# Two of the four channel-mix down products computed by two levels of the seven-product scheme

## The chip, the cores and the metric

The kernel runs on one core of a Trainium2 chip. The metric is device time in microseconds, the median of several executions. TensorE (PE in the profile) multiplies, VectorE (DVE) adds, subtracts and normalises, ScalarE (ACT) does activations and copies out of PSUM, GpSimd (POOL) and SyncE (SP) mostly issue DMAs here.

## The reference, cut to what matters

The input is 2048 tokens of 512 features, in float32. The reference does a layer norm and then an RWKV layer: a time mix (four 512x512 products) and a channel mix, followed by a feed-forward part (FFN).

```python
kk = (h * cm_mk + hh * (1 - cm_mk)) @ Wkey.T     # 512 -> 2048
kv = jax.nn.silu(kk) @ Wval.T                    # 2048 -> 512, the channel mix's down product
sr = jax.nn.sigmoid((h * cm_mr + hh * (1 - cm_mr)) @ Wcr.T)
x = x + sr * kv
...
gate_up = jnp.einsum('bsh,oh->bso', h_shard, w_gate_up)
gate, up = jnp.split(gate_up, 2, axis=-1)
out = jnp.einsum('bsi,hi->bsh', silu(gate) * up, w_down)   # the FFN's down product
```

## The kernel before, in words

The tokens are cut into four blocks of 512 (`b` = 0 to 3). For each block the time mix and the channel mix run first, for all blocks; only then comes the FFN, again block by block. The residual of each block goes through device memory (`resid`) between the two parts.

**The scheme.** A product of two 512x512 matrices is done on 2x2 blocks of 256 with seven block products in place of eight (a Strassen-Winograd scheme). It needs four sums of the weights' blocks (S1 to S4) and four of the activations' blocks (T1 to T4). `unit` (L526) does this: each of its `product` calls issues four 128x256 matmuls per weight, and `unit` has seven products. `down_unit` (L977) is such a unit with four weights (WVAL to WVAL+3), since the inner dimension is 2048: 7 x 4 x 4 = 112 matmuls of 128x256. `down_product` (L1114), used by the FFN's down product alone, goes a second level down: each of the seven products (steps n = 0 to 6, `DOWN`) is itself split in quarters of 128 and done by seven products of four 128x128 matmuls, so 7 x 7 x 4 = 196 matmuls. Its operands need sums of quarters of the activations (`quarter_sums`, L1103: four subtractions of 128x512 per step, in the order T1, T2, T4, T3), and the results are put together from `u` tiles by `rest`, `seventh` and `summed`. In a step the order of the products is: A11, A12, then S2 with T2 (`third`), S4, S1 with T1 (`fifth`), S3 with T3 (`sixth`), A22 with T4 (`seventh`). `sixth` and `seventh` are put off and issued between the first products of step n+1.

**Weight sums.** `prepare` (L143) loads four pieces of a weight to SBUF through GpSimd's queue, makes four sums on VectorE and stores them to scratch in device memory. The list of such items (`preps`: `early`, then WK, WR, WV, WO, then `late`) is worked off a little at every `tick`, as `credit` allows. Weights and sums reach TensorE through SyncE's queue and a ring of 12 tiles (`ring`).

**What sets the order.** The program writes out the order of TensorE, VectorE and ScalarE by hand. Each engine runs its own instructions strictly in that order. After each product `tick` (L290) adds `SHARE` = 0.88 of the product's time to a budget, `slack`, from which the costs of VectorE's instructions (`cost`: 0.135 us and 1.07 ns per element of a partition) are taken; while the budget is positive, `tick` issues one more piece of pending work: a weight sum, else a step of the `hot` queue (sums of activations), else of the `background` queue (norms and mixes). Work that belongs to a product, such as putting a result together, is issued with that product whatever the budget. If a product needs something that hasn't been issued, it is issued on the spot (`need`, L314, or `run_one(True)`). `ffn_in` (L1006) is one of the background items: it makes the input of the FFN's block: four residual adds, the moments, a reciprocal root by Newton steps, four scalings, transposes on TensorE, four sums. For block 0 it is pushed just before the last `down_unit`.

The activations of the channel mix's down product lie in separate tiles of 128x2x256 (`q_tile`), one per group `g` of 512 hidden features; those of the FFN's lie in one tile for all four groups, so that a quarter sum there is one instruction for four groups.

Of the kernel before, what the change touches and what calls it, by code (L numbers as in the profile page):

```python
# [9 lines left out]
F32 = mybir.dt.float32  # L10
# [10 lines left out]
HB = TB // 2  # L21
EPS = 1e-5
PLAIN = 2
WAIT = 5
# [35 lines left out]
def rwkv_ffn_kernel(  # L60
# [3 lines left out]
    vecs: bass.AP,  # L64
    w: bass.AP,
    wd: bass.AP,
    out: bass.AP,
# [11 lines left out]
    up = ctx.enter_context(tc.tile_pool(name="up", bufs=6))  # L79
    small = ctx.enter_context(tc.tile_pool(name="small", bufs=3))  # L80
    ps = ctx.enter_context(tc.tile_pool(name="ps", bufs=6, space=bass.MemoryType.PSUM))
    pv = ctx.enter_context(tc.tile_pool(name="pv", bufs=1, space=bass.MemoryType.PSUM))
# [5 lines left out]
    htp = mixes.enter_context(tc.tile_pool(name="htp", bufs=2))  # L88
    prep = mixes.enter_context(tc.tile_pool(name="prep", bufs=6))
    pools = {"q": mixes.enter_context(tc.tile_pool(name="qp", bufs=30))}  # L90

# [27 lines left out]
    for n in range(NW):  # L119
        sources[n], sums[n] = parts(n), scratch(f"sum{n}", 4)  # L120
    for k in range(4):
        sources["d", k] = [wd[q, k] for q in range(4)]
        sums["d", k] = scratch(f"d{k}", 4)
    for q in (A11, A12, A22, S1, S2, S3, S4):
        sources["dd", q] = [wd[q, k] if q < 4 else sums["d", k][q - 4] for k in range(4)]
        sums["dd", q] = scratch(f"dd{q}", 4)

# [15 lines left out]
    def prepare(n, own):  # L143

        raw = []
        for k in range(4):
            t = prep.tile([P, 2, HB], F32, tag="raw", name="raw") if own else q_tile("q")
            paced(nc.gpsimd.dma_start(flat(t), sources[n][k]))
            raw.append(t)
        yield 1  # L150
        a11, a12, a22, a21 = raw
        for k, o, i0, i1, op in (
            (0, a22, a21, a22, ALU.add),
            (2, a21, a11, a21, ALU.subtract),
            (1, a11, a22, a11, ALU.subtract),
            (3, a12, a12, a11, ALU.subtract),
        ):
            tt(o, i0, i1, op)
            nc.gpsimd.dma_start(sums[n][k], flat(o))
            yield  # L160

    def ring(src):
        t = wring.tile([P, 2, HB], F32, tag="w", name="w")
        nc.sync.dma_start(flat(t), src)
        return t
# [6 lines left out]

    def down_weight(q, k):

        if k >= 4:
            need_sums(("dd", q))
            src = sums["dd", q][k - 4]
        elif q >= 4:
            need_sums(("d", k))
            src = sums["d", k][q - 4]  # L180
        else:
            src = wd[q, k]
        return ring(src).rearrange("p a (h c) -> p (a h) c", c=P)
# [64 lines left out]
    def prep_one():  # L248
        item = preps[0]
        if item[1] > 0:  # L250
            return False
        try:
            if next(item[2]) is not None:
                item[1] = WAIT
        except StopIteration:
            preps.popleft()
            finished.add(("sums", item[0]))
            if len(preps) > 1 and item[3] > 1:
                begin(preps[1])
            elif preps:  # L260
                begin(preps[0])
        return True
# [7 lines left out]
    def prepare_all(ns, own, depth):  # L270
        empty = not preps
        for n in ns:
            preps.append([n, 0, prepare(n, own), depth, False])
        if empty:
            for item in list(preps)[:depth]:
                begin(item)

    def need_sums(n):
        while ("sums", n) not in finished:
            begin(preps[0])  # L280
            preps[0][1] = 0
            prep_one()

    def due():
# [672 lines left out]
    def up_unit(b, g):  # L957
# [3 lines left out]
        def sink(i, j, c):  # L961
            t = q_tile("s")
            nc.scalar.activation(t, c, AF.Silu)
            s[i, j] = B[(B11, B12, B21, B22)[2 * i + j]] = t

# [11 lines left out]
    def down_unit(b):  # L977
# [6 lines left out]
        def done():  # L984
            nc.sync.dma_start(resid[b], x1s.pop(b))

        unit(
            [WVAL + g for g in range(4)],
            [Lazy((b, g)) for g in range(4)],
            sink,  # L990
            True,
            done,
            loose=b == NB - 1,
        )

# [51 lines left out]
    def ffn_up(b, g):  # L1047
        s = gated.pop((b, g))
        hid = hidden.setdefault(b, {})

        def sink(i, j, c):
            q = (B11, B12, B21, B22)[2 * i + j]
            if q not in hid:
                hid[q] = hidden_tile()
            tt(hid[q][:, g], c, s[i, j], ALU.mult)
            if g == 3:
                made.add((b, q))
                if q in (B11, B22):
                    quarter_sums(b, 0 if q == B11 else 1)

        def done():
            if g == 0:
                for t in (T1, T2, T4):
                    hid[t] = hidden_tile()
            urgent((b, "f", g), sums_of({t: hid[t][:, g] for t in hid}))
            if g == 3:
                made.update((b, t) for t in (T1, T2, T4, "T3"))

# [4 lines left out]

    hidden, made, asked = {}, set(), set()
    room = {}
# [5 lines left out]
    def last_room():  # L1081

        room["hidden"] = ctx.enter_context(tc.tile_pool(name="hidden", bufs=7))
        pools["q"] = ctx.enter_context(tc.tile_pool(name="fq", bufs=15))
        more = ctx.enter_context(tc.tile_pool(name="more", bufs=1))
        m, _ = op_tile("quads")
# [4 lines left out]

    def quarters(t):
        return {2 * k + m: t[:, :, k, m * P : (m + 1) * P] for k in range(2) for m in range(2)}

    def quarter_operand(b, n):

        x = quarters(hidden[b][DOWN[n][1]])
        new = room["sets"][n % 2]
        x[T1], x[T2], x[T4] = new[:3]
        x["T3"] = new[3] if n < 2 else x[B12]  # L1100
        return x

    def quarter_sums(b, n):  # L1103
        x = quarter_operand(b, n)
        asked.add((b, n))

        def run():
            for o, i0, i1 in (T1, B12, B11), (T2, B22, T1), (T4, B21, T2), ("T3", B22, B12):
                tt(x[o], x[i0], x[i1], ALU.subtract)
                yield  # L1110

        urgent((b, "quarters", n), run())

    def down_product(b, sink, final):  # L1114
        base = {}

        def summed(n, r):
# [28 lines left out]
            else:  # L1146
                add("u2", "u2")
                sink(1, 0, base["u2"])

        def steps(n):  # L1150
# [3 lines left out]
            st = {}  # L1154
            x = quarter_operand(b, n)

            def product(dst, q, k, first):
                if k in (T1, T2, T4, "T3"):
                    while (b, n) not in asked:
                        flush_one()  # L1160
                    while (b, "quarters", n) not in finished:
                        run_one(True)
                wt = down_weight(a, q)
                for g in range(4):
                    mm = nc.tensor.matmul(  # L1165
                        dst,
                        lhsT=x[k][:, g, :],
                        rhs=wt[:, g, :],
# [42 lines left out]
            def seventh():  # L1211
# [3 lines left out]
                if n + 2 < 7:  # L1215
                    quarter_sums(b, n + 2)
                summed(n, r)
# [4 lines left out]
        for n in range(7):  # L1222
            t = DOWN[n][1]
            while (b, t if t != T3 else "T3") not in made:
                flush_one()
            one = steps(n)
# [6 lines left out]
            for k in range(2, 5):  # L1233
                one[k]()
                tick(half)
                if n == 0:
                    pop_held()
            held.extend((half, k) for k in one[5:])

    def ffn_down(b):  # L1240
# [12 lines left out]

        down_product(b, sink, final)

    early = [WCR] + [WKEY + g for g in range(4)] + [WVAL + g for g in range(4)]
    late = [n + g for g in range(4) for n in (WG, WU)] + [("dd", A11)]
    late += [("d", k) for k in range(4)] + [("dd", q) for q in (S4, S2, A12, S1, S3, A22)]  # L1260

# [27 lines left out]
    for b in range(NB):  # L1289
# [6 lines left out]
        if b + 1 < NB:  # L1296
            out_unit(b + 1)
        need((b, "ck"))
        if nxt:
            push(f"norm{b + 2}", time_norm(b + 2))  # L1300
        for g in range(4):
            up_unit(b, g)
            if b == 1 and g == 0:
                credit[1] = 0.55
            if g == 0:
# [14 lines left out]
        if nxt:  # L1320
            for n, u in (("k", k_unit), ("r", r_unit), ("v", v_unit)):
                u(b + 2)
    while preps:
        need_sums(preps[-1][0])
    mixes.close()
    last_room()
    for b in range(NB):
        for g in range(4):
# [16 lines left out]
def _layout(inputs):  # L1345
# [30 lines left out]
    )  # L1376
    def quarter_quarter(i, j, m, k):
        at = slice(i * HB + m * P, i * HB + (m + 1) * P)
        lo = j * HB + k * P

        q = [down[at, g * H + lo : g * H + lo + P].T for g in range(4)]
        return np.stack(q, axis=1).reshape(P, 4 * P)

    places = ((0, 0), (0, 1), (1, 1), (1, 0))
    wd = np.stack(
        [np.stack([quarter_quarter(i, j, m, k) for m, k in places]) for i, j in places]
    )
    return {
        "x": x,
        "vecs": np.ascontiguousarray(vecs),  # L1390
        "w": np.ascontiguousarray(w),
        "wd": np.ascontiguousarray(wd),
    }
# [19 lines left out]
```

## Time and profile before

| | |
|---|---|
| median of three runs | 1256.66 us (1255.7 to 1257.06) |
| profiled execution, time / span | 1256.11 / 1254.3 us |
| PE busy | 1238.0 us, 99% |
| DVE busy | 702.6 us, 56% |
| ACT busy | 355.8 us, 28% |
| channel mix's fourth down product (`down_unit(3)`) | about 627 to 679 us from the start, other units' matmuls between |
| FFN | from 679 us |
| FFN's down product of block 0 | about 774 to 823 us |

An fp32 matmul stands in the records as two matmul instructions, so counts of records are halved to get matmuls. In a timeline a line is: start in us, duration in us, engine, source line, operation, output<-input, count, and in brackets how long the engine sat idle before and what released it.

### The profile page before, as it was taken

Reading aid. Unit: us, or ns where it says so; the run is one execution under the profiler, and the core shown is the slowest. Engines: PE = TensorE matmul, PEld = TensorE weight load, DVE = VectorE, ACT = ScalarE, POOL = GpSimd, SP = SyncE. Lnnn points to the kernel's source line nnn. Section 1 sums busy time; section 2 is a strip of 40 time slices with the busy share of each in tenths; the row PEclk is TensorE's granted clock in tenths of the full one; section 3 lists DMA queues with packets and bytes.
Section 4 is the critical chain, followed back from the end, with each engine's and each line's share of the span. In section 5 each row is a group of like instructions: output and inputs, shape, how many; then the busy total and the mean of one; then the engine's idle time right before and its main releaser. Section 6 shows DMA issues by size and latency. Waiting matters only on the chain.

```text
span 1254.3 us, 18161 instructions
## 1 busy us (share of the span) xinstructions
PE 1238.0 (99%) x6588; PEld 1109.2 (88%) x6588; DVE 702.6 (56%) x1319; ACT 355.8 (28%) x656; POOL 151.1 (12%) x276
## 2 busy tenths in 40 slices
PE   8999999999999999999999999999999999999998
PEld 7888888888888888888888888998899988998898
DVE  5867566467674665722562265555546455462466
ACT  5433263142522334302311232212221132212211
POOL 2122221222121222222210000000000000000000
PEclk9999999999999999999999999999999999999999
DMA  5666777888778877798865655895559855785575
GB/s 188 233 195 211 244 249 244 249 292 282 241 259 257 290 251 248 248 334 309 254 211 178 221 145 151 247 345 164 144 173 302 280 151 150 234 291 165 152 220 200
DMA packets 137959, 288.55 MB, mean 230 GB/s; under 512 B 17296, under 2 KB 18320, under 8 KB 136848
## 3 DMA queue, kind: packets, MB, share of 16 engines
q1 hardware_dynamic: 115424, 215.53, 56.1%
q0 software_dynamic: 21440, 70.27, 15.4%
q10 hardware_dynamic: 1008, 1.59, 0.3%
q8 instruction: 53, 0.87, 0.3%
q14 instruction: 34, 0.28, 0.1%
HBM read 245.39 MB, written 41.94 MB: 229 GB/s over the span
## 4 chain that ended last, share of the span: by engine, by line
PE 95%; ACT 3%; DVE 2%; issue 1%; DMA 0%; POOL 0%; ACTq 0%; DVEq 0%; POOLq 0%
PE ps L546 49%; PE ps L1165 14%; PE accv L546 11%; PE accx L546 10%; PE ps L656 8%; PE ps L430 2%; ACT mix L483 1%; PE warm L337 1%; DVE u L379 1%; DVE mix L387 0%; DMA w<-in_w 0%; ACT e L877 0%; ACT x L740 0%; ACT r L878 0%; ACT accv L564 0%
## 5 line engine op out<-in xcount | busy, mean ns | idle before, releaser
L546 PE MATMUL ps<-zT,w 128*128 128x256 f32 x1280 | 289.5, 379 | 0.7 <-ACT u L574 0.7
L546 PEld LDWEIGHTS ps<-zT,w 128*128 128x128 f32 x1280 | 241.8, 190 | 33.2 <-ACT u L574 1.1
L546 PE MATMUL ps<-mix,w 128*128 128x256 f32 x880 | 201.0, 379 | 0.0
L546 PEld LDWEIGHTS ps<-mix,w 128*128 128x128 f32 x880 | 167.0, 190 | 22.6
L379 DVE TENSOR_TENSOR u<-u,accx 128x512 f32<-128x512 f32 x64 | 43.9, 686 | 118.3 <-ACT accx L578 118.3
L1165 PE MATMUL ps<-w,hid 128*128 128x128 f32 x832 | 104.7, 275 | 0.4 <-ACT r L1177 0.4
L1165 PEld LDWEIGHTS ps<-w,hid 128*128 128x128 f32 x832 | 99.8, 192 | 1.3 <-ACT r L1177 0.5
L546 PE MATMUL ps<-w,t 128*128 128x256 f32 x432 | 96.5, 379 | 0.0
L546 PEld LDWEIGHTS ps<-w,t 128*128 128x128 f32 x432 | 81.9, 190 | 11.1
L1165 PE MATMUL ps<-w,quads 128*128 128x128 f32 x704 | 89.2, 275 | 0.4 <-ACT r L1177 0.4
L656 PE MATMUL ps<-mix,w 128*128 128x256 f32 x384 | 85.1, 380 | 3.7 <-DVE mix L387 3.7
L656 PEld LDWEIGHTS ps<-mix,w 128*128 128x128 f32 x384 | 72.3, 190 | 14.6 <-DVE mix L387 5.1
L1165 PEld LDWEIGHTS ps<-w,quads 128*128 128x128 f32 x704 | 84.3, 192 | 0.9 <-ACT r L1177 0.5
L379 DVE TENSOR_TENSOR u<-ps,u 128x512 f32<-128x512 f32 x65 | 44.9, 691 | 66.3 <-PE ps L546 66.3
L578 ACT COPY accx<-ps 128x512 f32<-128x512 f32 x64 | 36.5, 571 | 153.0 <-PE ps L546 152.9
L379 DVE TENSOR_TENSOR raw<-raw 128x512 f32<-128x512 f32 x92 | 63.3, 688 | 29.1 <-DMA raw<-d 10.0
L564 ACT COPY accv<-ps 128x512 f32<-128x512 f32 x64 | 36.5, 571 | 140.5 <-PE ps L546 140.5
L1177 ACT COPY r<-ps 128x128 f32<-128x128 f32 x112 | 29.8, 266 | 142.7 <-PE ps L1165 142.7
L574 ACT COPY u<-ps 128x512 f32<-128x512 f32 x64 | 37.5, 585 | 112.9 <-PE ps L546 112.9
L1249 POOL DMA_DIRECT2D out<-resid x12 | 8.6, 716 | 476.9 <-DVE resid L379 476.9
L546 PE MATMUL accv<-zT,w 128*128 128x256 f32 x256 | 60.7, 380 | 0.7 <-ACT accv L564 0.7
L546 PE MATMUL accx<-zT,w 128*128 128x256 f32 x256 | 60.5, 379 | 0.0
(158 smaller groups left out, 1659.1 us busy)
## 6 DMA issues: line engine op xcount, KB each, us to landing
w<-sum SPq DMA_DIRECT2D x304, 256.0 KB, 3.3
w<-in_w SPq DMA_DIRECT2D x256, 256.0 KB, 3.3
w<-dd SPq DMA_DIRECT2D x112, 256.0 KB, 3.6
raw<-in_w POOLq DMA_DIRECT2D x48, 256.0 KB, 4.8
sum<-raw POOLq DMA_DIRECT2D x48, 256.0 KB, 3.8
w<-d SPq DMA_DIRECT2D x48, 256.0 KB, 3.3
q<-in_w POOLq DMA_DIRECT2D x36, 256.0 KB, 4.9
sum<-q POOLq DMA_DIRECT2D x36, 256.0 KB, 3.9
```

The costliest lines, as they stand in the source:

```text
L337: nc.tensor.transpose(pt[:, 0, 0:P], ident, ident)
L379: nc.vector.tensor_tensor(out, a, b, op)
L430: nc.tensor.transpose(flat[:, t * P : (t + 1) * P], h[:, t, c * P : (c + 1) * P], ident)
L483: nc.scalar.activation(dst(c), hT[:, c, 0:TB].rearrange("p (j t) -> p j t", j=2), AF.Copy, scale=onem[:, row - MK, c : c + 1],)
L546: mm = nc.tensor.matmul(pz[:, m, :], lhsT=lhsT, rhs=rhs, start=first and g == 0 and m == 0 and k == 0, stop=g == last and k == 1, skip_gro ...
L564: nc.scalar.copy(accv, acc["z"])
L574: nc.scalar.copy(tmp["u2"], acc["z"])
L578: nc.scalar.copy(accx, acc["z"])
L656: mm = nc.tensor.matmul(acc[i, j][:, m, :], lhsT=act[:, k, lo] if by_token else wg[:, k, lo], rhs=wg[:, k, :] if by_token else act[:, k, : ...
L1165: mm = nc.tensor.matmul(dst, lhsT=x[k][:, g, :], rhs=wt[:, g, :], start=first and g == 0, stop=g == 3, skip_group_check=True,)
L1177: nc.scalar.copy(st["r"][:, m, n * P : (n + 1) * P], st["z"])
L1249: eng.dma_start(out_t[b][:, 2 * j : 2 * j + 2, i * HB : (i + 1) * HB], rs[b][:, 2 * j : 2 * j + 2, i * HB : (i + 1) * HB],)
```

## The change

For blocks 2 and 3 (`TWO` = 2) the channel mix's down product goes through `down_product` instead of `unit`. For that:

- a second layout of the value weights, `wv`, in quarters of 128, is given to the kernel next to `w`; the first-level sums of the value weights are stored in a different layout (`vals`), from which quarters are read as four pieces of 128 elements per partition;
- seven more items of weight sums, `("v", "q", q)`, are prepared on the chip, ahead of those of the FFN; credit for weight sums rises from 0.55 to 0.7 per tick after block 1's first up unit, is 0 inside the two new down products and 0.9 after them; what is left of the list at the end of the mixes is done in the FFN, except items already begun, which are finished on the spot (`finish`);
- the quarter sums of the channel mix's activations are issued per group: 16 subtractions of 128x128 per step in place of four of 128x512;
- `set_room` takes one of the three operand tiles (`op_tile`) for the quarter sums from block 2 on, `qp` shrinks from 30 to 29 tiles;
- in `down_product`, `have_operand` waits for operands per group.

```diff
-    for k in range(4):
+
+    vals = [
+        dram.tile([4, P, 2 * HB], F32, tag=f"val{k}", name=f"val{k}").rearrange(
+            "g p (k m c) -> g p k m c", k=2, m=2
+        )
+        for k in range(4)
+    ]
+    for g in range(4):
+        sums[WVAL + g] = [v[g].rearrange("p k m c -> p (k m c)") for v in vals]
+    fine = {}
+    for k, (m, kk) in enumerate(places):
         sources["d", k] = [wd[q, k] for q in range(4)]
         sums["d", k] = scratch(f"d{k}", 4)
+        for q in range(4):
+            fine["d", q, k] = wd[q, k]
+            fine["d", 4 + q, k] = sums["d", k][q]
+            fine["v", q, k] = wv[q, k]
+            fine["v", 4 + q, k] = vals[q][:, :, kk, m, :].rearrange("g p c -> p g c")
+    for f in "vd":
+        for q in (A11, A12, A22, S1, S2, S3, S4):
+            sources[f, "q", q] = [fine[f, q, k] for k in range(4)]
+            sums[f, "q", q] = scratch(f"{f}q{q}", 4)
...
     def prep_one():
...
+            item[5] += 1
+            if item[5] == 2 and item[3] == 1 and len(preps) > 1:
+                begin(preps[1])
...
+    def finish(n):
+        item = preps.popleft()
+        for _ in item[2]:
+            pass
+        finished.add(("sums", n))
...
     def up_unit(b, g):
...
+            if b >= TWO and g == 3 and q in (B11, B22):
+                quarter_sums(("v", b), 0 if q == B11 else 1)
...
     def down_unit(b):
...
-        unit([WVAL + g for g in range(4)], [Lazy((b, g)) for g in range(4)], sink, True, done, loose=b == NB - 1)
+        if b >= TWO:
+            credit[1] = 0.0
+            down_product("v", b, sink, done, loose=b == NB - 1)
+            credit[1] = 0.9
+        else:
+            unit([WVAL + g for g in range(4)], [Lazy((b, g)) for g in range(4)], sink, True, done)
...
-    def quarter_sums(b, n):
-        x = quarter_operand(b, n)
-        asked.add((b, n))
+    def quarter_sums(u, n):
+        asked.add((u, n))
         def run():
+            x = quarter_operand(u, n)
             for o, i0, i1 in (T1, B12, B11), (T2, B22, T1), (T4, B21, T2), ("T3", B22, B12):
-                tt(x[o], x[i0], x[i1], ALU.subtract)
+                for xg in x:
+                    tt(xg[o], xg[i0], xg[i1], ALU.subtract)
                 yield
...
-    late = [n + g for g in range(4) for n in (WG, WU)] + [("dd", A11)]
-    late += [("d", k) for k in range(4)] + [("dd", q) for q in (S4, S2, A12, S1, S3, A22)]
+    late = [("v", "q", q) for q in (A11, S4, S2, A12, S1, S3, A22)]
+    late += [n + g for g in range(4) for n in (WG, WU)] + [("d", k) for k in range(4)]
+    late += [("d", "q", q) for q in (A11, S4, S2, A12, S1, S3, A22)]
...
+        if b == TWO:
+            set_room()
...
             if b == 1 and g == 0:
-                credit[1] = 0.55
+                credit[1] = 0.7
...
-    while preps:
-        need_sums(preps[-1][0])
+    while preps and preps[0][4]:
+        finish(preps[0][0])
+    del pools["raw"]
     mixes.close()
     last_room()
+    if preps:
+        begin(preps[0])
```

## The prediction

> **What bounds the kernel now.** I read the page first, then busy time by stretches, then the timeline of single engines in the two stages that matter: the channel mix's last down product, and the FFN's down product, which already has the form that the change introduces. The page's first part:
>
> ```profile
> PE 1238.0 (99%) x6588; PEld 1109.2 (88%) x6588; DVE 702.6 (56%) x1319; ACT 355.8 (28%) x656; POOL 151.1 (12%) x276
> ```
>
> TensorE is the bound, with 16 us of idle time in the whole span. So the change can gain only by giving TensorE less to do, and loses wherever it makes TensorE wait. The stretches say how much room VectorE has in the stage that is changed:
>
> ```profile
> 575.00:600.00 25.00, 25.00 (x117) 22.02 (x116) 8.21 (x12) 7.66 (x13) 5.42 (x10) 1.00 0.89 305
> ```
>
> The columns are stretch, its length, then busy time of PE, PEld, DVE, ACT, POOL, the granted clock, DMA share and GB/s. PE is full and DVE busy 8.2 of 25 us: there is room on average. What matters below is where in the order the work stands.
>
> TensorE's pace, one level (PE alone, around the last down product):
>
> ```profile
> 648.15 1.91 PE L430 MATMUL ps<-ident,z 128*128 128x128 f32 x16
> 649.89 1.89 PE L546 MATMUL accv<-w,s 128*128 128x256 f32 x8
> 651.62 7.07 PE L546 MATMUL ps<-w,t 128*128 128x256 f32 x32
> 658.53 7.07 PE L546 MATMUL ps<-w,s 128*128 128x256 f32 x32
> ```
>
> From 651.62 to 658.53 there are 32 records, 16 matmuls: 0.432 us each. The first line is the transposes of the FFN's block 0: its input is made inside this down product, so it costs no wait today. VectorE in the FFN's down product:
>
> ```profile
> 799.88 0.29 DVE L379 TENSOR_TENSOR r<-ps,r 128x128 f32<-128x128 f32 x1 [2.45 <-PE ps L1165]
> 800.09 0.68 DVE L379 TENSOR_TENSOR quads<-hid 128x512 f32<-128x512 f32 x1
> ...
> 806.14 0.29 DVE L379 TENSOR_TENSOR r<-ps,r 128x128 f32<-128x128 f32 x1 [2.46 <-PE ps L1165]
> ...
> 812.39 0.29 DVE L379 TENSOR_TENSOR r<-ps,r 128x128 f32<-128x128 f32 x1 [2.46 <-PE ps L1165]
> 812.79 0.69 DVE L379 TENSOR_TENSOR r<-r 128x512 f32<-128x512 f32 x1
> 813.40 0.69 DVE L379 TENSOR_TENSOR quads<-hid 128x512 f32<-128x512 f32 x1
> ```
>
> The 128x128 `r` add is the first thing after `seventh`, so its period, 6.255 us (12.51 over two), is a step of 28 matmuls: 0.2234 us each, 0.894 per product. VectorE waits 2.46 us for TensorE in each step. From one start to the next an independent instruction follows a 128x128 one after 0.21 us and a 128x512 one after 0.61; one that needs the result before it follows after 0.40 and about 0.73, as in the scaling of the block's result:
>
> ```profile
> 666.43 0.69 DVE L387 SCALAR_TENSOR_TENSOR sr<-sr,u 128x512 f32<-128x512 f32 x1
> 667.16 0.69 DVE L387 SCALAR_TENSOR_TENSOR x<-sr,x 128x512 f32<-128x512 f32 x1
> ```
>
> **The change, part by part.**
>
> **(a) TensorE's work, removed and added.** Per block 112 x 0.432 = 48.4 us go and 196 x 0.2234 = 43.8 come: -4.6, for two blocks **-9.2 us**. The arithmetic falls by an eighth, but the small matmul's pace gives part of it back. ScalarE's extra copies (28 per block, 0.27 us each in the FFN) hide behind products of 0.9 us.
>
> **(b) Quarter sums that are late.** A step now has 16 subtractions of 128x128 in place of four of 128x512. By their true pace that is 16 x 0.21 = 3.4 us against 2.7, and VectorE would have room. But the planner charges 0.272 each, 4.35 per step; with `rest`, `seventh` and the sink (up to 3.0) that exceeds its budget of 0.88 x 6.0 = 5.3. So it puts the sums off, and in the built order of the changed program those of steps 4, 5 and 6 stand behind the work of the `seventh` just before the product that needs them. In steps 5 and 6 T2 is issued only there, with no TensorE work between `seventh` of n-1 and `third` of n. Step 5, from the end of `seventh`: 0.2 until VectorE sees it, `r` 0.40, two adds 0.73 each, `sr` 0.73, `x` 0.61, the first T2 subtraction 0.29, back to TensorE 0.06: 3.75 us. TensorE waits only for the first group; the others come every 0.21 us, faster than its matmuls. Step 6: 0.2 + 0.40 + 0.73 + 0.73 + 0.61 + 0.61 + 0.29 + 0.06 = 3.63. Step 4: T3 is ready 3.86 after `seventh`, `sixth` is due 4 products (3.57) after: 0.3. Steps 0 to 3 have their sums in time. Per block 7.7, for two **+15.3 us**. If nothing of VectorE's order held, 0; with each 128x128 at its full 0.29, +17.
>
> **(c) The mix of block 3.** `set_room` holds an operand tile, so the `ck` mix of block 3 starts only when block 2's is freed, and is issued at `need`, after the last `seventh` of block 2's down product. That ends one product (1.7) before `up_unit(3, 0)`: 0.2 + 0.40 + 0.73 + 0.73 + 0.61, then two mixes of 0.75 (row of 128x512 mixes, 748 ns): TensorE waits about **+2.0 us**. Between 0 and 3.
>
> **(d) The tail of block 3's down product.** Its `sixth` and `seventh` have no next step to stand between. The same happens at the kernel's end today:
>
> ```profile
> 1245.80 1.06 PE L1165 MATMUL ps<-w,quads 128*128 128x128 f32 x8
> 1247.21 1.16 PE L1165 MATMUL ps<-w,hid 128*128 128x128 f32 x8 [0.35 <-ACT r L1177]
> ```
>
> 1.41 and then 1.52 us (the next starts at 1248.73) for products of 0.89: **+1.1 us**.
>
> **(e) The FFN's input loses its cover.** In the changed order the planner finds no budget for `ffn_in(0)` in block 3's down product. All of it stands on VectorE behind the last `seventh`, and behind five weight sums that `finish` issues; the transposes stand on TensorE behind all its products. From the end of `seventh`: result 0.2 + 0.40 + 0.73 + 0.73 + 0.61 = 2.7; five weight sums, three of them dependent, 3.4; four residual adds of 0.61, 2.4; then the moments and the root:
>
> ```profile
> 729.15 0.69 DVE L393 BATCH_NORM_STATS2 st<-resid 128x6 f32<-128x512 f32 x1
> 729.87 0.18 DVE L394 BATCH_NORM_AGGREGATE mv<-st 128x2 f32<-128x6 f32 x1
> 729.97 0.67 DVE L393 BATCH_NORM_STATS2 st<-resid 128x6 f32<-128x512 f32 x1
> ```
>
> four pairs of 0.82, 3.3; twelve tiny dependent instructions 0.2 apart, 2.4 (both starts and the scaling follow):
>
> ```profile
> 642.80 0.16 DVE L387 SCALAR_TENSOR_TENSOR rstd<-a,rstd 128x4 f32<-128x4 f32 x1
> 643.00 1.46 DVE L383 TENSOR_SCALAR z<-resid,mv,rstd 128x512 f32<-128x512 f32 x3
> ```
>
> four scalings 1.9. Together 16.1, with the way back **+16.2 us**; nothing else is on TensorE's order to cover it. The transposes themselves were paid before too. The loads for the five sums and the residual have been issued a hundred microseconds or more ahead of it, or at least one whole down product, so I add no DMA.
>
> **(f) The clock after idle.** The start of the kernel shows what a cold TensorE costs:
>
> ```profile
> 1.36 6.91 PE L337 MATMUL warm<-ident 128*128 128x128 f32 x44 [1.36 <-POOL ident masks.py:199]
> 8.11 1.06 PE L343 MATMUL accv<-ident 128*128 128x128 f32 x8
> ```
>
> 44 records in 6.75 us, where the warm pace (x8 in 0.89) makes 4.9: 1.85 lost. The row does not say when it recurs; no wait today is over 1.6 us. [...] By the row alone I would add nothing; [...] **+1.9 us** after (e), and for (b)'s waits of 3.7 us[...] little: 0 to 1.9 each, I take 0.5 for all four. The profile's granted clock reads 1.00 at the start too, so it will not show this; the pace will.
>
> [...]
>
> **(g) More weight sums.** Seven items of 4 loads, 4 sums and 4 stores: 28 x 0.69 = 19 us of VectorE, in stages where PE is the bound and DVE was 50 to 85% busy, plus 14.7 MB. Per new down product 49 ring loads stand in for 28. The FFN runs the same 49 at a DMA share of 0.9 without a wait. But 12 of the 49 read pieces of 512 bytes. On SyncE's queue a packet of about 1.9 KB takes 97 ns (115424 packets, 56.1% of 16 engines): if 512 bytes go at the same bytes per time, nothing changes; if a packet costs the same whatever its size, such a tile takes 3.1 us against 0.8, and steps 1-2 and 4-5 outrun the ring's lead by some 4 us per block. The trace has no such row. I take +1.0 in all for (g), between 0 and 8.
>
> **Sum.** -9.2 + 15.3 + 2.0 + 1.1 + 16.2 + 1.9 + 0.5 + 1.0 = +28.8. The profiled execution (1256.11, span 1254.3) becomes 1284.9; on the runs' median of 1256.66: **1285.5 us**.
>
> **The rivals.**
> - *Late sums cost nothing* (T2 reaches TensorE in time; the planner's lateness is only on paper). For it: VectorE's 2.46 us of idle time per step in the FFN. Against it: in steps 5 and 6 the order leaves no other place. Without (b): 1270.
> - *Transfers and the clock add more*: each 3.7 us wait also cools TensorE (4 x 1.85 = 7.4), and short pieces cost 8: 1285.5 + 6.9 + 7 = 1299. For it: a DMA share of 0.9 in such stages; against it: [...] they give the ring time.
> - *Faster*: one mechanism, VectorE's order does not bind, because it is idle enough to do `ffn_in` and T2 as soon as their inputs exist. At the border of mixes and FFN it would save (e) and (f), in the steps (b), and (c): 35.9 together, 1250. It decides from the point where four fifths of that, 28.8, are hidden. Against it: an engine runs its instructions in order, and the `r` add in front waits for `seventh`.
> - *The change does not do what it says*: no; in the built order both blocks have 49 products of four 128x128 matmuls. 1257, a chance of 1%.
>
> **How the numbers follow.** The forecast 0.70, its own range 1280 to 1292; late sums free 0.10 (1262 to 1279); more transfers and clock 0.14 (1292 to 1306); faster 0.05; unchanged 0.01. From 1273 to 1298 about 0.85 of this lies, with the bounds of (b), (c) and (g). A measurement of this kernel tells about 0.2%, 2.5 us, from no change. Faster 0.05, within 0.01, slower 0.94.
>
> **What would show it.** In the profile after: PE idle before quarter-sum matmuls of 3.7 us twice per new down product; one PE wait of about 16 us before transposes of `z` at the start of the FFN, followed by some 3 us at half pace; 2 us before the first up unit of block 3; a pace of 6.26 us per step elsewhere. (a) is wrong if a step without a wait takes longer than 6.3. The whole is wrong if that one wait is missing or PE waits for ring tiles.

## The result, and the profile after

The changed kernel takes 1324.65 us (median of six, 1318.29 to 1326.35) against 1256.18 before: a ratio of 1.0539, 95% interval 1.0517 to 1.056. The forecast was 1285.5 with a range up to 1298; the sign was right, the size was not: +68.5 us in place of +28.8. The profiled execution has a span of 1322.8 us against 1254.3, 68.5 more.

The page's first part, and the longest of what TensorE waited for (in total, times, longest, in us):

```profile
PE 1254.1 (95%) x6924; PEld 1129.9 (85%) x6924; DVE 783.1 (59%) x1621; ACT 367.0 (28%) x705; POOL 184.2 (14%) x332
```

```profile
PE accv L588 <- ACT accv L606: 20.2, 6, 8.3
PE ps L472 <- DVE z L425: 14.7, 1, 14.7
PE ps L1243 <- DVE quads L421: 14.0, 4, 3.6
PE ps L472 <- DVE h L425: 4.2, 5, 1.6
```

The second line is the FFN's uncovered input (e), the third the four late T2 (b): 14.7 and 14.0 us of idle time, near the forecast of 16.2 and 15.3 (the table below counts the whole loss of each). The first and the fourth were not in the forecast. And TensorE is busy 16 us longer, although it was given less to do. The timeline of TensorE in step 5 of block 2's new down product shows why:

```profile
574.63 1.06 PE L1243 MATMUL ps<-w,quads 128*128 128x128 f32 x8
579.25 2.07 PE L1243 MATMUL ps<-w,quads 128*128 128x128 f32 x8 [3.56 <-DVE quads L421]
581.11 1.91 PE L1243 MATMUL ps<-w,s 128*128 128x128 f32 x8
582.82 1.86 PE L1243 MATMUL ps<-w,quads 128*128 128x128 f32 x8
584.52 1.06 PE L1243 MATMUL ps<-w,t 128*128 128x128 f32 x8
```

A product takes 0.894 us from start to start; the three after the wait take 1.86, 1.71 and 1.70. The stretches show the granted clock (after POOL's column) in these 5.25 us and just after:

```profile
579.25:584.50 5.25, 5.25 (x24) 5.25 (x25) 2.16 (x11) 0.27 (x1) 0.00 (x0) 0.50 0.24 59
584.50:588.00 3.50, 3.50 (x34) 3.50 (x32) 1.52 (x6) 0.80 (x3) 0.00 (x0) 1.00 0.71 224
```

After the wait the granted clock is 0.50, from 584.50 us on 1.00 again. At the start of the FFN, TensorE alone:

```profile
727.51 1.16 PE L1243 MATMUL ps<-w,quads 128*128 128x128 f32 x8 [0.36 <-ACT r L1255]
743.35 4.31 PE L472 MATMUL ps<-ident,z 128*128 128x128 f32 x16 [14.68 <-DVE z L425]
```

From 727.51 to 743.35 is 15.84 us where the product needs 0.89: 14.95 lost. The transposes after this wait run at a granted clock of 0.50 (743.35 to 747.40 us).

**Where the rest went.** In the mixes there is a new kind of wait. GpSimd's queue, VectorE and TensorE at one such place (three views of the same stretch):

```profile
425.49 0.55 POOL L190 DMA_DIRECT2D sum<-raw  x1 [0.27 <-issue]
427.92 0.55 POOL L190 DMA_DIRECT2D sum<-raw  x1
434.46 0.54 POOL L179 DMA_DIRECT2D raw<-in_w  x1 [6.00 <-DMA sum<-raw]
```

```profile
439.78 0.69 DVE L421 TENSOR_TENSOR raw<-raw 128x512 f32<-128x512 f32 x1 [8.10 <-issue]
```

```profile
446.01 3.78 PE L588 MATMUL accv<-mix,w 128*128 128x256 f32 x8 [8.34 <-ACT accv L606]
```

A load of the next weight item waits 6.0 us for the landing of a store of the item before, because it takes over that store's raw tile. The store is the one of 425.49: it took 8.7 us to land. The load lands 5.2 us after its issue, at 439.70. VectorE, which has a weight sum next in its order, stands still for 8.1 us until then (its row names no releaser, but the sum starts 0.1 us after the landing); ScalarE stands behind VectorE's work, and TensorE waits 8.3 us for ScalarE's copy. TensorE's product after the wait is at half pace again (3.57 us for 1.73, granted clock 0.50 from 446.01 to 449.50 us).

Taking the start of each group of matmuls to the next start, less the number of matmuls times the undisturbed pace, the 68.5 us divide like this:

| | forecast | measured |
|---|---|---|
| (a) TensorE's own work, two down products | -9.2 | -9.2 (steps without a wait take 6.26 us) |
| (b) late quarter sums | +15.3 | 14.6 for T2, 0.3 for T3 |
| (c) mix of block 3 | +2.0 | 2.3 |
| (d) tail of block 3's down product | +1.1 | 1.15 |
| (e) the FFN's first input | +16.2 | 14.95 |
| (f) half pace after (e) | +1.9 | 2.8 |
| (f) half pace after (b) and (c) | +0.5 | 8.7 after (b), 2.0 after (c) |
| (g) weight sums, with the half pace after their waits | +1.0 | 30.9, at five places (2.6, 3.8, 10.1, 5.0, 8.8) and 0.5 |
| sum | +28.8 | +68.5 |

### The profile page after: what moved, and what is told of

Read it like the earlier page. It is cut to its first block, busy times and chain, and to the rows that moved or that the text cites. A ratio compares the mean times of both kernels' runs of the same rounds, so it can differ in the third digit from the quotient of the medians.

```text
span 1322.8 us, 19460 instructions
## 1 busy us (share of the span) xinstructions
PE 1254.1 (95%) x6924; PEld 1129.9 (85%) x6924; DVE 783.1 (59%) x1621; ACT 367.0 (28%) x705; POOL 184.2 (14%) x332
## 4 chain that ended last, share of the span: by engine, by line
PE 76%; DMA 9%; issue 7%; DVE 5%; ACT 2%; POOL 2%; POOLq 0%; ACTq 0%; DVEq 0%
PE ps L588 33%; PE ps L1243 21%; PE ps L698 8%; PE accv L588 7%; PE accx L588 7%; PE ps L472 2%; DMA sum<-raw 2%; DMA raw<-in_w 1%; DMA raw<-val 1%; DVE raw L421 1%; DMA raw<-d 1%; POOL raw L179 1%; DMA raw<-in_wd 1%; DMA dq<-raw 1%; DMA raw<-in_wv 1%
## 5 line engine op out<-in xcount | busy, mean ns | idle before, releaser
L588 PE MATMUL ps<-mix,w 128*128 128x256 f32 x880 | 204.7, 384 | 2.1 <-DVE mix L429 2.1
L1243 PE MATMUL ps<-w,quads 128*128 128x128 f32 x1056 | 140.2, 283 | 14.7 <-DVE quads L421 14.0
L1243 PEld LDWEIGHTS ps<-w,quads 128*128 128x128 f32 x1056 | 131.6, 198 | 16.4 <-DVE quads L421 14.8
L421 DVE TENSOR_TENSOR raw<-raw 128x512 f32<-128x512 f32 x116 | 79.6, 686 | 64.1 <-issue 31.8
L1255 ACT COPY r<-ps 128x128 f32<-128x128 f32 x168 | 44.7, 266 | 232.0 <-PE ps L1243 232.0
L1243 PE MATMUL ps<-w,hid 128*128 128x128 f32 x832 | 104.7, 275 | 0.4 <-ACT r L1255 0.4
L1243 PEld LDWEIGHTS ps<-w,hid 128*128 128x128 f32 x832 | 99.8, 192 | 1.3 <-ACT r L1255 0.5
L698 PE MATMUL ps<-mix,w 128*128 128x256 f32 x384 | 85.1, 380 | 3.7 <-DVE mix L429 3.7
L421 DVE TENSOR_TENSOR r<-ps,r 128x256 f32<-128x256 f32 x84 | 30.1, 358 | 70.5 <-PE ps L1243 65.8
L588 PE MATMUL accv<-mix,w 128*128 128x256 f32 x176 | 45.9, 407 | 19.5 <-ACT accv L606 19.5
```

The source lines that it names most:

```text
L421: nc.vector.tensor_tensor(out, a, b, op)
L588: mm = nc.tensor.matmul(pz[:, m, :], lhsT=lhsT, rhs=rhs, start=first and g == 0 and m == 0 and k == 0, stop=g == last and k == 1, skip_gro ...
L698: mm = nc.tensor.matmul(acc[i, j][:, m, :], lhsT=act[:, k, lo] if by_token else wg[:, k, lo], rhs=wg[:, k, :] if by_token else act[:, k, : ...
L1243: mm = nc.tensor.matmul(dst, lhsT=x[g][k] if f == "v" else x[0][k][:, g, :], rhs=wt[:, g, :], start=first and g == 0, stop=g == 3, skip_gr ...
L1255: nc.scalar.copy(st["r"][:, m, n * P : (n + 1) * P], st["z"])
```

## The experiments

All are edits of the changed kernel. Theory after the profile was read: three causes, the weight sums (g), the late quarter sums with the halved clock after them (b, f), and the FFN's uncovered input (e); each can be taken away alone.

**The weight sums alone.** `TWO` = 4, so all four down products stay with `unit`; the new sums are made and not used.

```diff
-TWO = 2
+TWO = 4
...
-            unit([WVAL + g for g in range(4)], [Lazy((b, g)) for g in range(4)], sink, True, done)
+            unit([WVAL + g for g in range(4)], [Lazy((b, g)) for g in range(4)], sink, True, done, loose=b == NB - 1)
...
-        if b == TWO:
+        if b == 2:
             set_room()
```

> All of the change but its point: all four down products go through the one-level unit as before, while the seven new items of weight sums, their rate, the early begin of the next item and the held operand tile stay (the sums of quarters of the value weights are made and not used). Theory: the weight sums alone cost about 30 us, because two items share six raw tiles, the loads wait on GpSimd's queue for the landing of the item before's stores, and VectorE then waits in order for the loads. Expected 1284 us (1275 to 1293), with waits of several us of VectorE before raw sums. Rival (the loss belongs to the new down products and their transfers): 1256 to 1263.

Measured: 1289.28 us, ratio to before 1.0257 (1.024 to 1.0275). The sums alone cost 33 us, half of the whole loss. TensorE's longest waits here:

```profile
PE accv L588 <- ACT accv L606: 18.1, 7, 8.9
PE ps L588 <- ACT accx L620: 5.9, 1, 5.9
```

**Eight raw tiles.**

```diff
-        "raw": mixes.enter_context(tc.tile_pool(name="prep", bufs=6)),
-        "q": mixes.enter_context(tc.tile_pool(name="qp", bufs=29)),
+        "raw": mixes.enter_context(tc.tile_pool(name="prep", bufs=8)),
+        "q": mixes.enter_context(tc.tile_pool(name="qp", bufs=27)),
```

> The changed kernel with eight raw tiles in place of six (and 27 q tiles in place of 29), so that two items of weight sums never share one; the order of TensorE, VectorE and ScalarE stays. Theory (shared raw tiles): the waits of loads for stores go, and with them some 25 of the 31 us: 1298 us (1292 to 1306). Rival (rate of the sums and load on the DMA engines): 1315 or more.

Measured: 1303.13 us, 21.5 us less than the changed kernel. GpSimd's waits of loads for stores, and VectorE's waits for raw tiles that are left:

```profile
POOL raw L179 <- DMA d<-raw: 0.6, 1, 0.6
```

```profile
DVE raw L421 <- issue: 17.0, 6, 6.8
DVE raw L421 <- DMA raw<-d: 13.2, 3, 6.7
DVE raw L421 <- DMA raw<-in_w: 8.5, 4, 2.8
```

The waits of loads for stores are gone (0.6 us in all; 78 in the changed kernel), yet VectorE still waits for loads, and TensorE behind it, at two of the five places (3.7 and 7.5 us, with 1.5 of half pace after each) and for 1.4 us at a third. So about half of (g) is gone, some 16 of the 31 us. The profiled executions differ by 20.3 us; the other 4 us lie in the half pace after (b) and (c), which was milder in this run (the last section shows one such place). The reuse of the raw tiles is about half of the cause, not all of it. At the later of the two places GpSimd issues, and VectorE starts the sum:

```profile
623.18 1.60 POOL L179 DMA_DIRECT2D raw<-in_wd  x3
627.10 0.54 POOL L179 DMA_DIRECT2D raw<-in_wd  x1 [2.32 <-issue]
633.25 0.69 DVE L421 TENSOR_TENSOR raw<-raw 128x512 f32<-128x512 f32 x1 [6.85 <-issue]
```

VectorE was ready at 626.40, before the last load was even issued. (This place lies behind the first new down product, where the credit is 0.9 and the planner puts an item every 9.6 us.) At the earlier place the loads were issued from 418.0 to 420.2 us, VectorE was ready at 425.6, and the last load landed at 428.8. The loads start too shortly before the sum that needs them.

**The next item begun late.**

```diff
             item[5] += 1
-            if item[5] == 2 and item[3] == 1 and len(preps) > 1:
-
-                begin(preps[1])
```

> The changed kernel without the early begin: the next item's loads are issued only when the item before is done, as before the change. By the theory of the shared raw tiles the waits for stores go (-25 to -30), but the order of VectorE changes with it: quarter sums of steps 3 and 4 are then issued late too, which costs some 4 us per new down product, and more items are left for the FFN: 1304 us (1296 to 1312). Rival (rate and load on the DMA engines): 1315 or more.

Measured: 1301.72 us. In the mixes only 3.4 us of (g) is left, at one place; another 3.8 us appear in the FFN's first down product, where TensorE waits 1.9 us for a quarter sum at 854 us. As expected T2 is late in steps 3 and 4 too: waits of 0.6, 1.4 and 2.8 us in block 2 and 2.8 in block 3. Items now follow each other every 17 us in place of every 12, so this run alone does not tell the raw tiles from the rate.

**The same, without the new down products.** The weight sums alone, with the edit just shown.

> As the run of the weight sums alone (all four down products by the one-level unit, the sums of the value weights' quarters made and not used), but with the next item begun only when the item before is done. Theory (the early begin, with six raw tiles for two items, is what costs): 1260 us (1257 to 1265). Rival (28 more loads and 28 more stores of 256 KB and the higher rate cost by themselves): 1275 or more.

Measured: 1256.44 us, ratio 1.0004 (0.9996 to 1.0013). At this slower rate loads, sums and stores of the same kind cost nothing that can be measured. Up to the FFN 27 items go through the raw tiles here, against 30 in the run of the weight sums alone; the others are done in the FFN.

**The weight sums alone, at the old rate.** The run of the weight sums alone, with the early begin kept and this edit; by the planner items then come every 15 us in place of 12.

```diff
-                credit[1] = 0.7
+                credit[1] = 0.55
```

> As the run of the weight sums alone (one-level unit for all down products, early begin of the next item kept), but with the credit left at 0.55 per tick as before the change, so that items follow each other every 15 us in place of 12. If the shared raw tiles cost whenever two items are in flight, about half or more of the 33 us stays, since a store and a load still take some 10 us after the second sum: 1272 us (1266 to 1285). If the rate alone is the cause (the chain of store and load fits once items are slower): 1256 to 1262.

Measured: 1256.81 us, ratio 1.0003 (0.9994 to 1.0012). My reading of the raw tiles falls in the form that I gave it. GpSimd's waits for stores, here and in the changed kernel, TensorE's longest waits here, and VectorE's waits for one kind of load in the run of the weight sums alone (credit 0.7) and here (0.55):

```profile
POOL raw L179 <- DMA sum<-raw: 32.8, 13, 6.0
```

```profile
POOL raw L179 <- DMA sum<-raw: 37.9, 13, 6.0
```

```profile
PE accv L588 <- ACT accv L606: 3.6, 4, 1.0
```

```profile
DVE raw L421 <- DMA raw<-d: 32.6, 4, 14.1
```

```profile
DVE raw L421 <- DMA raw<-d: 6.5, 1, 6.5
```

The loads wait for stores just as long (75 us over all items against 78 in the changed kernel; the first of these rows stood at 2.0 us before the change). As many items as at 0.7, 30, go through the raw tiles. But VectorE's idle time before raw sums is 30.0 us in all, as before the change (29.1), against 109.3 at 0.7, and TensorE pays nothing for it.

What costs is the time that the rate leaves. The loads of an item are issued at the second sum of the item before. From there to the landing of the last load it takes, on average over the items from 320 to 640 us, 12.2 us at 0.7 and 12.1 at 0.55: other stores go out, they land after some 5 us, the loads behind them land after some 5 more (medians at 0.7: 5.1 us for `sum<-raw`, 5.4 for `raw<-in_w`). VectorE is ready for the sum that needs them after 8.0 us at 0.7 and after 11.8 at 0.55. (In the changed kernel it is 12.0 against 9.6, with eight raw tiles 10.6 against 9.0.) The mean DMA share in that stretch is 0.88 at 0.7 and 0.89 at 0.55, so the mean load on the DMA engines does not tell the two apart.

**Work for TensorE inside the waits.** 24 records of needless matmuls ahead of the T2 products of steps 5 and 6. They leave the accumulator `accx` in another state, which changes sums that later products add onto it, so the output is no longer the layer's; the order and the number of the kernel's own instructions stay, and the run is read for its time alone.

```diff
+                if f == "v" and n in (5, 6) and q == S2:
+                    for k4 in range(4):
+                        for _ in range(3):
+                            nc.tensor.matmul(
+                                flat(accx)[:, k4 * P : (k4 + 1) * P],
+                                lhsT=ident,
+                                rhs=ident,
+                                start=True,
+                                stop=True,
+                                skip_group_check=True,
+                            )
                 wt = down_weight(f, a, q)
```

> The changed kernel with 12 needless 128x128 matmuls (2.7 us at the full pace) on TensorE just ahead of the T2 products of steps 5 and 6, inside the waits of 3.6 us[...]. Theory (the pace after these waits is halved by the idle time): the four losses of 1.6 to 2.8 us after the waits go, 8.7 together: 1316 us (1313 to 1320), the waits no shorter. Rival (the pace has another cause, as the operands or the accumulation): 1324 or slower.

Measured: 1316.36 us (1313.42 to 1319.19), 8.3 less than the changed kernel, for more work. TensorE at the place shown above:

```profile
575.65 2.84 PE L1244 MATMUL accx<-ident 128*128 128x128 f32 x24
579.37 1.16 PE L1254 MATMUL ps<-w,quads 128*128 128x128 f32 x8 [0.88 <-DVE quads L421]
580.37 1.06 PE L1254 MATMUL ps<-w,s 128*128 128x128 f32 x8
```

The T2 product starts 3.72 us after the slot that it had, as before the edit (3.73). But it and the two products after it take 1.00, 0.89 and 0.89 us from start to start, where they took 1.86, 1.71 and 1.70 at a granted clock of 0.50; the mean clock of this run's executions is 0.982 to 0.984, of the changed kernel's 0.974 to 0.980. Idle time just ahead of them had made these products slow.

**The quarter sums ahead of the block's result.**

```diff
             def seventh():
+                if f == "v":
+                    while (u, n + 1) in asked and (u, n + 1) not in finished:
+                        run_one(True)
                 product(st["z"], A22, T4, False)
```

> The changed kernel, but whatever is left of the quarter sums of step n+1 is issued ahead of the last product (seventh) of step n, and so ahead of the block's result on VectorE. Theory: the four waits of 3.6 us before T2 and the half pace after them (14.6 + 8.7 us) go: 1301 us (1298 to 1306). Rival (VectorE has no room in these steps: its 16 small subtractions per step and the result take longer than a step's 6.25 us): the wait moves to another product and less than half of it is gained, 1313 or more.

Measured: 1301.45 us, 23.2 less (14.6 + 8.7 = 23.3 expected). There is no `L1243 <- DVE quads` among TensorE's waits any more:

```profile
PE accv L588 <- ACT accv L606: 19.0, 7, 8.1
PE ps L472 <- DVE z L425: 14.1, 1, 14.1
PE ps L588 <- DVE mix L421: 4.6, 2, 3.4
PE ps L472 <- DVE h L425: 4.1, 3, 2.8
```

VectorE had the room; only the place in its order was wrong.

**The FFN's first input ahead of the last down product.**

```diff
+            if b == NB - 1 and g == 0:
+                push((0, "z", "t"), ffn_in(0), op_free)
...
         if b == NB - 1:
-            push((0, "z", "t"), ffn_in(0), op_free)
+            need((0, "z"))
         down_unit(b)
```

> The changed kernel with the FFN's first input (adds, moments, root, scalings, transposes) handed to the planner after block 3's first up unit and asked for before its down product, in place of behind it. Theory: the wait of 15 us at the start of the FFN and 2.7 us of slow pace after it go; the four sums of that input still stand behind the five weight sums, which leaves a wait of some 4 us there: 1311 us (1306 to 1316). Rival (the input's work delays the up units as much): 1320 or more.

Measured: 1310.42 us, 14.2 less (13.7 expected). The 15 us are gone. The transposes, now among the up units, wait 6.1 us for `z`, and a wait of 3.0 us for the input's sums is left.

**All three.** The late begin, the sums first and the input first.

> The changed kernel with all three: the late begin of the next item of weight sums, the quarter sums ahead of the last product of each step, and the FFN's first input ahead of the last down product. If the three causes are all there is, what stays is the gain of TensorE's smaller work (-9.2), the wait for the mix of block 3 (+2 and some slow pace), the tail (+1.1) and small waits of the first sums (+3): 1253 us (1249 to 1260), about as fast as before the change or faster. If something else costs time too (as the transfers of 49 ring tiles per down product, a quarter of them in pieces of 512 bytes), 1263 or more.

Measured: 1252.73 us (1250.82 to 1253.84), ratio to before 0.9971 (0.996 to 0.9982). The page, and TensorE's longest waits:

```profile
PE 1229.4 (98%) x6924; PEld 1111.4 (89%) x6924; DVE 782.4 (63%) x1621; ACT 366.2 (29%) x705; POOL 184.3 (15%) x332
```

```profile
PE accv L585 <- ACT accv L603: 4.4, 4, 1.8
PE ps L695 <- DVE mix L426: 3.7, 4, 1.5
PE ps L1240 <- DVE quads L418: 1.7, 1, 1.7
```

TensorE is busy 8.6 us less than before the change, near the -9.2 of (a), and of that 3.6 us arrive at the end, 0.3% of the time. No wait for ring tiles is among its waits, so the 49 tiles per down product, a quarter of them in short pieces, do not cost TensorE anything here.

## Why the prediction was wrong, point by point

- **(a)** held: the pace read off the FFN's down product carries over. Had everything else been free, the change would have been worth 9 us.
- **(b), (c), (d), (e)** held, to about 1 us each. The order of VectorE in the built program, with starts taken from neighbouring rows, gave the waits: 3.75 and 3.63 us for T2 were 3.73 and 3.59. The removals (-23.2 with the half pace, -14.2) agree. (e) was 1.2 too long at its last term: it made the transposes wait for all four scalings, 1.9 us, but in the changed kernel the scalings start at 742.65 and the transposes at 743.35, after the first one. (c) came near in part by luck: its terms add to 4.17 us, 2.5 after the 1.7 of the product, where I wrote 2.0; in the trace TensorE waits for one mix, not two, and that mix starts 0.5 us late because of ScalarE.
- **(f)** was mis-sized at the four short waits: 0.5 was put for what measured 8.7, and 2.0 more came after (c). TensorE's longest wait in the trace of before is 1.6 us, so the trace did not show when the slow pace of the start comes back; that it would after (e), and hardly after waits of 3.7 us, I assumed. In the profiled execution the first product after each of the four takes 1.86 to 1.87 us for 0.894, and the pace fell after shorter waits too (below). I had 1.9 each as an upper bound; the four measured 1.5 to 2.8. Also wrong: that the granted clock would not show it. It reads 0.50.
- **(g)** is the step that failed: "+1.0 in all, between 0 and 8" measured 30.9; without that excess of 29.9 the time would have been 1295 us, inside the range. I costed the weight sums as VectorE's time and as bytes, both of which have room, and asked only of the ring whether loads come in time. I did not follow an item's own chain: the store has to land before the tile is loaded again, the load has to land before the sum, and the sum stands in order on VectorE ahead of what TensorE needs (at the place shown above 8.7 us for the store, 5.2 for the load, and 8.1 us in which VectorE stands still). The trace of before had the two durations (medians of 3.8 us for a store and 4.8 for a load, 8.6 together). Four of an item's five pieces (four sums and a closing step) lie between the start of the next item's loads and the sum that needs them; at 0.7 per tick of 1.72 us that is 9.8 us, an estimate from the program's constants. The margin of some 1 us was there to be seen; that the chain would take 12 us was not. The runs show that the rate decides: at 0.55 the same waits on GpSimd's queue are harmless. At the fast rate the reuse of the raw tiles is about half of the loss (some 16 of 31 us are gone with eight of them).
- **The rivals.** "Late sums cost nothing" is refuted by the run with the sums first. "Transfers and the clock add more" was nearest, though 1324.65 lies above its range too: its 7.4 us for the clock after the short waits were about right (8.7), but its transfers, the ring's short pieces, were the wrong ones. "Faster" needed VectorE's order not to bind; it binds (23.2 us less with the quarter sums at another place in it). With that order mended and the late begin, the kernel is 0.3% faster than before the change.

What stays open: why single loads and stores took 8 us and more at some places (5 us is the median), at a mean DMA share that is the same in the run at 0.55; whether other transfers of that moment or their own spacing made it so was not tried. Nor is it shown why VectorE's waits for loads of 30 us in all cost TensorE nothing, while 64 in the changed kernel cost it 31: at the slow rate VectorE has more time to catch up, with an item every 15 us in place of 12, but no run separates that from the length of the single waits.

## What to carry to other kernels

When background work shares an in-order engine with the critical path, cost it by its own chain (store lands, buffer is free, load lands, compute), not by its busy time alone, and set the chain against the time that the rate leaves between the start of the loads and the instruction that needs them. Here the same work cost nothing at 11.8 us for a chain of 12.1, and 33 us at 8.0 for 12.2. On an engine whose order is written out by a planner, read the built order at each hand-over and ask what stands in front of the operand; a planner that overcharges small instructions puts them off until they are late, however idle the engine is. And price a stall of TensorE at its length plus the half pace that can follow it: here 1.5 to 2.8 us after waits of 3.4 us and more, and once nothing.

## What the runs showed of the hardware that was not expected

The granted clock fell after a wait shorter than the four of (b), too. After the 2.1 us wait of (c), in a stretch of 4.00 us in which TensorE was busy for 1.95, the next stretch of the changed kernel ran at a mean granted clock of 0.69:

```profile
606.93 2.85 PE L588 MATMUL ps<-mix,w 128*128 128x256 f32 x8 [2.08 <-DVE mix L429]
```

```profile
606.93:612.40 5.47, 5.46 (x16) 4.21 (x17) 5.03 (x8) 1.57 (x3) 0.55 (x1) 0.69 1.05 402
```

The first two products after this wait take 2.66 and 2.82 us for 1.73. With eight raw tiles, after the same wait of 2.08 us, they take 2.06 and 1.73 (starts at 588.79, 590.85 and 592.58 us). And a longer wait need not do it. The two T2 waits of block 2 with eight raw tiles:

```profile
562.44 1.16 PE L1243 MATMUL ps<-w,quads 128*128 128x128 f32 x8 [3.56 <-DVE quads L421]
563.43 1.06 PE L1243 MATMUL ps<-w,s 128*128 128x128 f32 x8
...
572.39 2.08 PE L1243 MATMUL ps<-w,quads 128*128 128x128 f32 x8 [3.44 <-DVE quads L421]
574.26 1.92 PE L1243 MATMUL ps<-w,t 128*128 128x128 f32 x8
```

After 3.56 us of idle time the product takes 0.99 us and the granted clock is 1.00 (562.40 to 567.90 us), after 3.44 it takes 1.87 and the clock is 0.50 (572.40 to 577.60). What decides between the two is not shown, nor how much idle time is enough. The spread of the changed kernel's own times goes with it: its fastest execution, 1318.29 us, has a mean granted clock of 0.980, the other five, 1324.48 to 1326.35, of 0.974 to 0.976. A difference of 0.005 over 1320 us is 6.6 us by estimate, about the spread that was seen.
